# Attention scores turned onto pixels: fp32 products with a 0/1 matrix, or TensorE transposes with it

## The chip, the core and the metric

The kernel runs on one core of one Trainium2 chip, in one launch. The metric is the device time in microseconds (us) from the first to the last instruction. The engines are named as in the profile: PE is TensorE's matmul, PEld its weight load, DVE is VectorE, ACT is ScalarE, POOL is GpSimd, SP is the engine that issues most DMAs.

## The reference

The input is 16 images of 56 x 56 pixels with 384 channels, fp32. Two residual layers run over it:

```python
x = x + dilated_attention(_gn(x), w_qkv, w_proj, b_proj)
x = x + depthwise_conv(_gn(x), sign(w))      # 3 x 3, one filter per channel, signs of the weights
```

`_gn` is a group norm over 32 groups of 12 channels. The attention has 12 heads of 32 channels in three groups of four; group g looks at the 3 x 3 neighbours of each pixel at a distance of 1, 2 or 3. For each pixel and head that makes nine scores:

```python
attn = softmax(einsum('bgdn,bgdkn->bgnk', qg, ku) * scale)   # k: nine neighbours
out  = einsum('bgnk,bgdkn->bgnd', attn, vu)
```

## The kernel before

**Tiling.** Channels lie on partitions. An image is cut into 7 chunks of 8 rows, 448 pixels (`PX`), so there are 112 chunks. A chunk passes three stages: A (load, turn to channels-first, statistics), B (attention) and C (convolution, turn back, store). The three stages run at once on different chunks.

**Order.** Each piece of work is filed by `at(when, order, piece)` under a time slice and a rank in the slice; a chunk owns nine slices (`STEP`), and at the end (L856) all pieces are run in that order. The softmax ranks first in a slice, then scores, statistics, convolution, the weighing of values, queries, keys and values, the output product. This fixes the program's order. The queues in the trace depart from it in places: the compile-time scheduler places an instruction where it holds that its inputs are ready. On PE bursts are kept whole by `in_one_go`.

**Scores.** `query(g)` (L463) leaves 128 channels of queries in PSUM, `pq`. `score(i)` multiplies them on DVE by three shifted copies of the keys (L516, tile `t`). `score_rounds` (L501) sums the 32 channels of each head with a 0/1 matrix `sel`; its result `ps` has one partition per neighbour and head and 448 pixels along the row: neighbour p = 9 g + o lands on partitions 32 (p % 4) + 4 (p // 4) and the three after it.

**Softmax.** `softmax_1` copies `ps` to SBUF (`sT`, ACT, L533). Then PE brings 112 pixels at a time onto partitions (L536): four products, each with 112 columns of `sT` as the weights and the 0/1 matrix `permf` as the moving operand, all four into one PSUM bank, tile `pt_s`. `permf` also puts the 108 scores of a pixel into the order that the softmax wants (`place`). DVE takes the maximum (L541, `mx`), subtracts it (L542, into `ew`), ACT takes the exponential (L543). Later slices normalise (L547 to L549), split the weights into three bf16 terms and turn them back to rows by a transposing DMA (`aT`).

**Weighing.** `weigh(i)` spreads three weights over the 32 channels of their heads on PE (L582, `pb_a`, only one buffer), DVE multiplies by the values (L589, `w`), POOL adds up (L597, L600, L601). `out_project` (L615, `po`) is the output product; DVE adds bias and residual (L618).

**Buffers.** `pt_s`, `pkv`, `po`, `pc`, `pt_x`, `pt_o` and the small tiles of the norm share the three PSUM buffers of `ps_mt` under the tag `mt`; a new tile waits until the readers of the tile that had its buffer are done.

**Other transposes.** The kernel already has TensorE transposes: `pt_x` in stage A (L412) and `pt_o` in stage C (L799), both fp32 with the identity matrix as the moving operand. L799 has the same shapes as L536: weights of 128 x 112, moving operand of 128 x 128.

**The matrix.** `perm` is built once at the start by POOL (L104 to L110): 27 selects, one for each neighbour of each group, set four ones each. Five blocks of four columns stay zero.

Of the kernel before, what the change touches and what calls it, by code (L numbers as in the profile page):

```python
# [17 lines left out]
P = 128  # L18
HEADS = 4
HD = 32  # L20
NG = 3
NTAP = 9
NQ = 4
ROWS = 8
SUB = 112
# [3 lines left out]
NPAD = 32  # L29
# [6 lines left out]
def dilated_attention_then_binary_conv(  # L36
# [28 lines left out]
    nc = tc.nc  # L65
# [10 lines left out]
    def place(p):  # L76

        g, o = divmod(p, NTAP)
        return NG * o + g
# [22 lines left out]

    perm = const.tile([P, NPAD, HEADS], F32, name="perm")
    nc.gpsimd.memset(perm, 0.0)  # L104
    for p in range(NG * NTAP):
        v = place(p)
        nc.gpsimd.affine_select(
            out=perm[:, v, :], in_=perm[:, v, :], compare_op=ALU.not_equal, fill=1.0,
            base=-(32 * (p % 4) + 4 * (p // 4)), pattern=[[-1, HEADS]], channel_multiplier=1,
        )  # L110
    permf = perm.rearrange("p v h -> p (v h)")
# [333 lines left out]
    def plan_b(m, t0):  # L445
# [78 lines left out]
        def by_neighbour(ap):  # L524
            return ap.rearrange("p s (o k) -> p s o k", o=NTAP)

        def over_neighbours(ap):
            return ap.unsqueeze(2).to_broadcast([SUB, NSUB, NTAP, GH])

        def softmax_1():  # L530

            sT = s_p.tile([P, PX], F32, tag="sT", name="sT")
            nc.scalar.copy(sT, had.pop("ps")[:, :PX])  # L533
            pt = ps_mt.tile([P, 512], F32, tag="mt", name="pt_s")
            for s in range(NSUB):
                nc.tensor.matmul(  # L536
                    pt[:SUB, s * P : (s + 1) * P], sT[:, s * SUB : (s + 1) * SUB], permf, start=True, stop=True
                )
            pt4 = pt[:SUB].rearrange("p (s v) -> p s v", s=NSUB)[:, :, :NR]
            mx = s_p.tile([SUB, NSUB, GH], F32, tag="mx", name="mx")  # L540
            nc.vector.reduce_max(mx, by_neighbour(pt4).rearrange("p s o k -> p s k o"), axis=AX.X)  # L541
            nc.vector.tensor_tensor(by_neighbour(weights), by_neighbour(pt4), over_neighbours(mx), ALU.subtract)  # L542
            nc.scalar.activation(weights, weights, AF.Exp, scale=SCALE)  # L543
# [95 lines left out]
        for i in range(9):  # L639
            at(t0 + i, SCORE, lambda i=i: score(i))  # L640
        at(t0 + 9, SOFTMAX, softmax_1)
        at(t0 + 10, SOFTMAX, softmax_2)
        at(t0 + 11, SOFTMAX, softmax_3)
# [243 lines left out]
```

## Time and profile before

| | |
|---|---|
| median of 3 runs | 5411.35 us (5409.35 to 5414.15) |
| profiled execution | 5405.2 us, granted TensorE clock 0.98 |
| DVE busy | 4150.0 us (77%), 4209 instructions |
| ACT busy | 2397.8 us (44%) |
| POOL busy | 4215.2 us (78%) |
| DMA queues, share of 16 engines | 54.2% and under 1% each |
| L536, PE | 896 matmuls of 273 ns, first at 102.1 us, last at 5182.5 us |
| L536, weight loads | 896 of 177 ns |
| `pt_s` read by L541 and L542 on DVE | 112 each, 0.60 us and 0.59 us |
| from one chunk's L536 to the next | 44.88 us in the plainest chunks, up to 50.66 us |

A group's row in the profile names the line, the engine and the operation, then what it writes and reads with shapes, how often it ran, its busy time and the mean time of one. A time of one instruction is from its start to its modelled end; matmuls overlap, so how much of PE a burst takes is read from the starts: the start of the next burst less its own. PE shows twice as many matmuls on L536 (896) as the program has products (448): each fp32 product runs as two instructions. Each transpose of L799 and L412 runs as one (1344 in either line, which is what the program has).

The idle time before a group is given with what ended it. The engine and the semaphore of that releaser are in the trace; the instruction named is the last one of that engine before the wait ended, and is not always the one that was needed.

The page's chain of work that ended last explains only a few per cent of this span, so it carries little here.

### The profile page before, as it was taken

The page shows a single profiled execution, that of the slowest core. Times are in us where ns is not written, and L with a number is a line of the kernel's source. Part 1 is how long each engine was busy: PE and PEld are TensorE (multiplying, and loading weights), DVE is VectorE, ACT ScalarE, POOL GpSimd, SP SyncE. Part 2 cuts the span into 40 slices and gives each one's busy share as a digit, 9 for nine tenths or more (in the row PEclk, how much of TensorE's full clock was granted, in tenths as well). Part 3 has the DMA queues.
Part 4 walks back from the last instruction along what each step waited for, and adds up shares of the span by engine and source line. Part 5 has one row for each costly group of instructions (what it writes and reads, how often), then busy time and mean ns, then how long its engine had stood idle before and what let it go on. Part 6 is the DMA issues. An engine that isn't in the chain of part 4 may idle for free. (4 is left out here: it accounts for less than half of the span.)

```text
span 5405.2 us, 77297 instructions
## 1 busy us (share of the span) xinstructions
PE 5205.9 (96%) x27669; PEld 2414.4 (45%) x27669; DVE 4150.0 (77%) x4209; ACT 2397.8 (44%) x4189; POOL 4215.2 (78%) x3049
## 2 busy tenths in 40 slices
PE   8999999999999999999999999999999999999965
PEld 4444444444444444444444444444444444444422
DVE  4887777878777787777777777787777778777754
ACT  3224444444444444444444444444444444444433
POOL 2677888888888887888888788888888888888880
PEclk9999999999999999999999999999999999999976
DMA  5444555655555555555655655555555655544443
GB/s 168 127 120 124 159 157 158 163 154 161 158 158 160 164 159 159 157 157 158 163 154 161 164 152 160 164 157 163 159 157 154 164 154 161 161 130 134 122 130 126
DMA packets 810799, 825.73 MB, mean 153 GB/s; under 512 B 359467, under 2 KB 800174, under 8 KB 810414
## 3 DMA queue, kind: packets, MB, share of 16 engines
q1 hardware_dynamic: 802430, 808.79, 54.2%
q10 hardware_dynamic: 7984, 12.00, 0.7%
q8 instruction: 219, 3.59, 0.3%
q14 instruction: 166, 1.36, 0.1%
HBM read 466.41 MB, written 231.21 MB: 129 GB/s over the span
## 5 line engine op out<-in xcount | busy, mean ns | idle before, releaser
L597 POOL TENSOR_TENSOR w<-w 128x1344 f32<-128x1344 f32 x672 | 2049.9, 3050 | 456.2 <-DVE w L589 396.7
L589 DVE TENSOR_TENSOR w<-pb_a,v 128x1344 f32<-128x1344 f32 x1008 | 1559.1, 1547 | 267.0 <-PE pb_a L582 177.4
L516 DVE TENSOR_TENSOR t<-pq,k 128x1344 f32<-128x1344 f32 x1008 | 1535.8, 1549 | 237.0 <-PE pq L463 236.1
L463 PE MATMUL pkv<-xn,wqkvT 128*128 128x448 f32 x3924 | 1569.9, 549 | 9.0 <-ACT xa L424 4.7
L463 PEld LDWEIGHTS pkv<-xn,wqkvT 128*128 128x128 f32 x3924 | 718.4, 190 | 671.8 <-issue 629.4
L615 PE MATMUL po<-y,wprojT 128*128 128x448 f32 x2016 | 834.9, 550 | 27.4 <-POOL y L601 15.0
L784 POOL TENSOR_TENSOR m<-m 128x1344 f32<-128x1344 f32 x210 | 644.7, 3070 | 274.1 <-ACT m L778 274.0
L463 PE MATMUL pq<-xn,wqkvT 128*128 128x448 f32 x1962 | 830.7, 558 | 0.0
L713 ACT ACTIVATE z<-z,mrz 96x448 f32<-96x448 f32 x840 | 578.3, 751 | 350.9 <-DMA z<-x1d 330.3
L501 PE MATMUL ps<-t,sel 128*32 128x448 f32 x6048 | 666.0, 550 | 26.0 <-DVE t L516 25.3
L778 ACT ACTIVATE m<-zg,ktap 128x448 f32<-128x448 f32 x945 | 555.5, 658 | 274.0 <-POOL m L784 266.9
L615 PEld LDWEIGHTS po<-y,wprojT 128*128 128x128 f32 x2016 | 376.4, 191 | 382.9 <-issue 341.1
L727 PE MATMUL pc<-z,kdiag 96*32 96x440 f32 (+1 forms) x5040 | 516.7, 543 | 6.4 <-POOL z L715 4.6
L463 PEld LDWEIGHTS pq<-xn,wqkvT 128*128 128x128 f32 x1962 | 344.0, 189 | 316.9 <-issue 316.9
L734 DVE TENSOR_TENSOR x<-pc,x 128x448 f32<-128x448 f32 x224 | 139.3, 622 | 353.2 <-PE pc L727 342.1
L582 PE MATMUL pb_a<-aT,spread 24*128 24x448 bf16 x3024 | 369.1, 359 | 32.2 <-DVE w L589 25.9
L601 POOL TENSOR_TENSOR y<-y,w 128x448 f32<-128x448 f32 x336 | 381.5, 1135 | 22.6
L618 DVE SCALAR_TENSOR_TENSOR xr<-po,bias,xr 128x448 f32<-128x448 f32 x336 | 227.5, 677 | 220.9 <-PE po L615 217.2
L600 POOL TENSOR_TENSOR y<-w 128x448 f32<-128x448 f32 x336 | 382.2, 1138 | 14.7
L473 ACT COPY v<-pkv 128x448 f32<-128x448 f32 x336 | 178.3, 531 | 484.1 <-PE pkv L463 475.8
L473 ACT COPY k<-pkv 128x448 f32<-128x448 f32 x336 | 178.2, 530 | 376.5 <-PE pkv L463 376.5
L501 PEld LDWEIGHTS ps<-t,sel 128*32 128x32 f32 x6048 | 170.6, 110 | 364.9 <-issue 247.8
(131 smaller groups left out, 4394.7 us busy)
## 6 DMA issues: line engine op xcount, KB each, us to landing
z<-x1d SPq DMA_DIRECT2D x570, 224.0 KB
xr<-xd SPq DMA_DIRECT2D x112, 672.0 KB
x1d<-xr SPq DMA_DIRECT2D x112, 672.0 KB
xn<-xd SPq DMA_DIRECT2D x109, 672.0 KB
xin<-in_x_dram SPq DMA_DIRECT2D x108, 672.0 KB
xd<-xa SPq DMA_DIRECT2D x315, 224.0 KB
out_dram<-osb SPq DMA_DIRECT2D x420, 168.0 KB
x<-x1d SPq DMA_DIRECT2D x112, 448.0 KB
```

The source lines that it names most:

```text
L463: nc.tensor.matmul(dst[:, :PX], wqkvT[:, cc, o0 : o0 + P], had["xn"][:, cc, :], start=(cc == 0), stop=(cc == NG - 1))
L501: return nc.tensor.matmul(had["ps"][32 * j : 32 * j + 32, :PX], sel[:, s0 : s0 + 32], tk, start=(issued[j] == 1), stop=(issued[j] == len(r ...
L516: nc.vector.tensor_tensor(t.rearrange("p k (r w) -> p k r w", w=W), q3, k3, ALU.mult)
L589: nc.vector.tensor_tensor(w.rearrange("p k (r w) -> p k r w", w=W), pb[:, :, :PX].rearrange("p k (r w) -> p k r w", w=W), three(kv[1][g][m ...
L597: nc.gpsimd.tensor_tensor(w0, w0, w, ALU.add)
L600: nc.gpsimd.tensor_tensor(y, w0[:, 0], w0[:, 1], ALU.add)
L601: nc.gpsimd.tensor_tensor(y, y, w0[:, 2], ALU.add)
L615: nc.tensor.matmul(po[:, :PX], wprojT[:, g, j * P : (j + 1) * P], had[f"y{g}"], start=(g == 0), stop=(g == NG - 1))
L713: nc.scalar.activation(z, z, AF.Identity, bias=mrz[:, j, q, 0:1], scale=mrz[:, j, q, 1:2])
L727: return nc.tensor.matmul(pcr[q * HD : (q + 1) * HD, :, lo:hi], kdiag[:, kx, j * NQ + q, :], rows(set_of(j, q))[:, :, lo + kx - 1 : hi + k ...
L778: nc.scalar.activation(rows(t[:, kx]), zp[:, ky : ky + ROWS, kx : kx + W], AF.Copy, scale=ktap[:, o : o + 1])
L784: nc.gpsimd.tensor_tensor(had["m"], had["m"], t, ALU.add)
```

## The change

The four products per chunk become four TensorE transposes with the same two operands: `sT` as the data, `permf` in the place of an identity. A transpose passes values through,[...] the five blocks of columns that were zero get ones as well, on the 20 rows of `ps` that no neighbour uses. That is five selects more at the start. The aim is to spend fewer PE instructions on a step that only moves numbers.

```diff
-    for p in range(NG * NTAP):
-        v = place(p)
+    for p in range(NPAD):
+        v = place(p) if p < NG * NTAP else p
         nc.gpsimd.affine_select(
             out=perm[:, v, :], in_=perm[:, v, :], compare_op=ALU.not_equal, fill=1.0,
             base=-(32 * (p % 4) + 4 * (p // 4)), pattern=[[-1, HEADS]], channel_multiplier=1,
@@ softmax_1
             for s in range(NSUB):
-                nc.tensor.matmul(
-                    pt[:SUB, s * P : (s + 1) * P], sT[:, s * SUB : (s + 1) * SUB], permf, start=True, stop=True
-                )
+                nc.tensor.transpose(pt[:SUB, s * P : (s + 1) * P], sT[:, s * SUB : (s + 1) * SUB], permf)
```

## The prediction

> **What bounds the kernel now.** I first read the busy shares and the slices, then a table by stretches, to see where PE sets the pace.
>
> ```profile
> PE 5205.9 (96%) x27669; PEld 2414.4 (45%) x27669; DVE 4150.0 (77%) x4209; ACT 2397.8 (44%) x4189; POOL 4215.2 (78%) x3049
> PE   8999999999999999999999999999999999999965
> ...
> 214.00:4767.00 4553.00, 4494.65 (x24051) 2091.40 (x24050) 3612.33 (x3625) 2082.99 (x3641) 3711.38 (x2577) 1.00 0.57 156
> 5200.00:5405.00 205.00, 119.75 (x672) 46.73 (x672) 79.48 (x126) 70.73 (x118) 53.04 (x58) 0.64 0.41 127
> ```
>
> The columns of the last two rows are the stretch, its length, then PE, PEld, DVE, ACT, POOL, clock, DMA share and GB/s. From 214 to 4767 us PE is busy 98.7% (4494.65 of 4553) at full clock, DVE and POOL about 80%. PE is the bound there; only the last 205 us, where PE is busy 58%, belong to others. So PE time taken away counts, except where PE then waits.
>
> Next, the groups by shape, for the price of what goes and of what comes:
>
> ```profile
> L536 PE MATMUL pt_s<-perm,sT 128*112 128x128 f32 x896 | 116.4, 273 | 2.5 <-ACT sT L533 2.5
> L799 PE MATMUL pt_o<-ident,xg 128*112 128x128 f32 x420 | 115.3, 274 | 0.0
> L536 PEld LDWEIGHTS pt_s<-perm,sT 128*112 128x112 f32 x896 | 112.8, 177 | 46.2 <-issue 41.7 <-ACT sT L533 4.2 <-ACT z L713 0.2
> L799 PEld LDWEIGHTS pt_o<-ident,xg 128*112 128x112 f32 x420 | 56.2, 134 | 0.0
> ```
>
> A pass of a product and a transpose of the same shape both show 273 ns; only the weight loads differ, 177 against 134 ns. What differs is the count, 8 per chunk against 4. As matmuls overlap, what they take is read from the starts, in the timeline of a plain chunk:
>
> ```profile
> 2635.34 1.04 PE L536 MATMUL pt_s<-perm,sT 128*112 128x128 f32 x8
> 2636.30 0.36 PE L582 MATMUL pb_a<-aT,spread 24*128 24x448 bf16 x3
> ...
> 2641.60 0.39 PE L799 MATMUL pt_o<-ident,x 128*112 128x128 f32 x2
> 2641.82 0.27 PE L799 MATMUL pt_o<-ident,xg 128*112 128x128 f32 x1
> 2642.02 0.36 PE L582 MATMUL pb_a<-aT,spread 24*128 24x448 bf16 x3
> ...
> 2642.79 1.71 PE L501 MATMUL ps<-t,sel 128*32 128x448 f32 x16
> ```
>
> Columns: start, length, engine, group. In all 105 chunks between 200 and 5000 us whose start the timeline shows, the L536 burst takes 0.97 us to the next start.
>
> Last, what DVE does at the same time:
>
> ```profile
> 2633.28 3.02 DVE L516 TENSOR_TENSOR t<-pq,k 128x1344 f32<-128x1344 f32 x2 [0.82 <-PE pq L463]
> 2636.22 0.68 DVE L618 SCALAR_TENSOR_TENSOR xr<-po,bias,xr 128x448 f32<-128x448 f32 x1
> 2636.81 0.60 DVE L541 TENSOR_REDUCE mx<-pt_s 112x48 f32<-112x432 f32 x1
> ...
> 2640.64 1.55 DVE L516 TENSOR_TENSOR t<-pq,k 128x1344 f32<-128x1344 f32 x1
> ```
>
> DVE starts when `pq` is there, 2.06 us ahead of `pt_s`, and then works without a gap until about 2645. Its reader of `pt_s` starts 0.43 us after the burst's end (2635.34 + 1.04), behind other DVE work. DVE does not wait for `pt_s`.
>
> **What the Trainium skill says.** "TensorE: Matmul & The Clock Gate", Terms, says that transpose mode is 4x faster for FP32. The trace agrees only in part: the products are two passes, the transposes of the same shape one, at the same pace. I take 2x. Part 4 of the page, PE-mode transpose, gives about 275 ns for one in a kernel's context; L799 shows 274 ns. It also says that transposes don't count as busy for the clock gate; half a microsecond of them in 45 us should do nothing, and the clock is 1.00 in the stretch above with 24 other transposes in each chunk. Part 2, step 1, says weight loads run ahead under the matmuls; the trace agrees, since loads of 134 ns fit matmuls that start 110 ns apart.
>
> **The change part by part.**
> 1. Removed: eight passes. (1.04 - 0.273) / 7 = 0.110 us from start to start, plus 0.20 us from the last to `pb_a`: 0.97 us.
> 2. Added: four transposes. The starts of L799 lie 0.11 us apart (0.39 - 0.273 = 0.117 for a pair; 2641.60 to 2641.82 is two), and the last one leaves 0.20 us to `pb_a`: 3 x 0.11 + 0.20 = 0.53 us. Change of mode: `pkv` takes 4.61 us ahead of `pt_x` as elsewhere, so 0. PE saves **0.44 us** per chunk, 49 us in 112. The bounds are 0.40 and 0.50.
> 3. What follows on PE. The spread `pb_a` (L582) needs the last product `w`, done 3.84 us before; its next one at +6.69 us from `pt_s` has 2.1 us to spare. The first tile of `pkv` finds a free buffer. The trace puts the second `pkv` tile's weight load down to DVE's L542 in 91 chunks, but I take the name for chance: the load starts on its usual beat of 0.375 us, and in the first chunk the same load starts before L542 is done. By rotation of three buffers `pt_x` needs the one of `pt_s`, with 2 us to spare.
> 4. Where it can be lost. The burst of scores `ps` (L501) at 2642.79 needs the third product `t`, which DVE ends at 2642.19. Hand-over takes 0.05 us (seen wherever PE waits for it). Spare: 0.60 - 0.05 = 0.55 us, more than 0.44. As DVE is tied to `pq`, which comes ahead of the change, it ends `t` no sooner; after this burst it idles until PE's `pc` and moves with PE again. So I read this spare in each of the 112 chunks. **66 have 0.44 or more and keep all: 29 us. The others keep about 1 us together**: in the chunks without convolution (to about 500 us) and in one or two of seven chunks in each image `ps` already waits or has under 0.3 us, and in one of seven PE waits 0.46 to 0.88 us for the norm on POOL, 2.2 us after `pt_s`:
>
> ```profile
> PE ps L501 <- DVE t L516: 17.4, 25, 1.5
> PE pv L331 <- POOL dev L325: 9.9, 12, 0.9
> ```
>
> (us, times, longest, from 200 to 4700 us.) There the 0.44 us only lengthens the wait.
> 5. The five selects cost POOL 0.14 us each (27 took 3.84 us): 0.7 us at the start. PE begins at 7.15 us, when the input lands, so I take 0 and keep 0.7 as the other end. `perm` is first read at 101.7 us. Readers, copies and DMAs stay as they are.
>
> Sum: 29 + 1 = 30 us, 5411 - 30 = **5381 us**.
>
> **The rivals.**
> - B, nothing is lost: DVE's order moves so that `t` is ready in time, or waits on POOL shift along. Then 49 us: 5362. For it: DVE has 20% free. Against it: the waits on `pv` and `t` are there.
> - C, a wait takes its place: the second `pkv` tile does wait for L542. L542 ends 3.11 us after the old start of `pt_s`, the load starts at 3.25; with 0.05 us for the hand-over only 0.09 us is left of 0.44. 66 x 0.09 = 6 us: 5405. For it: the 91 entries. Against it: the first chunk.
> - D, slower: DVE's order is not the program's (two products `t` of later slices stand ahead of L618 and L541), so the compiler may regroup it when `pt_s` is ready sooner. If the reciprocal (0.36 us) and a statistic (0.48 us) come ahead of the third `t`, it ends 0.84 us later, `ps` starts at 6.91 + 0.84 = 7.75 us instead of 7.45, and 66 chunks lose 0.3 us: 20 us, 5431. For it: with 0.11 us of spare left nothing may move. Against it: the order repeats exactly from image to image.
>
> **How the numbers follow.** My forecast 0.52, B 0.15, C 0.18, D 0.15. A and B are faster by over 0.2% (10.8 us): 0.67. C is within it: 0.18. D: 0.15. The range reaches from B (with 0.7 us to it, and the pace's bounds) to just past C, 5359 to 5411, and leaves out D.
>
> **What would show it.** Right: L536 with 448 matmuls and loads of about 134 ns; the burst 0.53 us to `pb_a`; plain chunks 44.44 us apart instead of 44.88; `ps` at +7.01 us; the `pv` waits about 1.3 us; PE's waits for `t` longer by 0.44 us where they were. Wrong: transposes that start further apart than 0.12 us (step 2); a second `pkv` tile off its beat (step 3, C); `ps` waiting in plain chunks, or another order on DVE (step 4, D); a first transpose later than 7.2 us (step 5).

## The result, and the profile after

The changed kernel takes 5559.26 us (median of 4 runs, 5556.49 to 5564.79), against 5411.3 us for the kernel before on the same chip: a ratio of 1.0274, 95% interval 1.0256 to 1.0292. It is **148 us slower**, where 30 us less was forecast. The profiled execution spans 5557.5 us, the one before 5405.2 us. The three lines of the call in the softmax have become one, so from L537 on the line numbers of this profile are two below those of before; the kernels of the experiments have shifts of a few lines of their own.

From the page, the busy shares; then the row of the stretch from 214 to 4767 us, with the columns that the prediction explains:

```profile
PE 5227.1 (94%) x27221; PEld 2378.0 (43%) x27221; DVE 4154.6 (75%) x4209; ACT 2381.2 (43%) x4189; POOL 4224.4 (76%) x3054
```

```profile
214.00:4767.00 4553.00, 4382.79 (x22916) 1999.13 (x22914) 3510.85 (x3515) 2002.26 (x3527) 3607.00 (x2498) 0.98 0.56 152
```

PE has 448 instructions fewer, as it should, and yet 21.2 us more busy time (5227.1 against 5205.9). Its idle time over the whole span went from 199.3 to 330.4 us (span less busy time), 131 us more. The two make up the 152 us between the spans. In the stretch PE is busy 96.3% instead of 98.7%, and its granted clock is 0.98 instead of 1.00. So there are two questions: what PE waits for, and why fewer instructions take longer.

The edited operation itself did what was forecast. Its matmuls (count, least, median and longest in ns, first and last start), and a plain chunk in the timeline:

```profile
L536 PE MATMUL pt_s<-perm,sT x448: 272/273/323, 102.0 to 5324.5; 128*112 128x128 f32 x150
```

```profile
2633.28 0.60 PE L536 MATMUL pt_s<-perm,sT 128*112 128x128 f32 x4
2633.81 0.36 PE L580 MATMUL pb_a<-aT,spread 24*128 24x448 bf16 x3
...
2640.29 1.71 PE L501 MATMUL ps<-t,sel 128*32 128x448 f32 x16
```

The burst now takes 0.53 us to the next start (2633.81 - 2633.28, and the same in 99 of the 101 chunks between 200 and 5000 us; of the 105 bursts of before, 103 take 0.97 us and two 1.06), its weight loads 133 ns each, and `ps` starts at +7.01 us. The next chunk starts 44.44 us later. All four numbers stand in the prediction. But such a chunk comes about once in each group of seven; most others take 45 to 52 us. In the kernel before 38 of the 111 intervals are the plain 44.88 us; the longest is 53.15 us, not 50.66 as the table above has it.

What PE waited for between 200 and 5000 us (us in total, times, longest):

```profile
PE pkv L463 <- ACT xa L424: 59.6, 13, 4.6
PE pv L331 <- POOL dev L325: 49.6, 14, 3.9
PE ps L501 <- DVE t L516: 45.3, 50, 2.0
```

The same in the kernel before:

```profile
PE ps L501 <- DVE t L516: 19.8, 28, 1.5
PE pv L331 <- POOL dev L325: 10.8, 13, 0.9
PE pkv L463 <- ACT xa L424: 4.7, 1, 4.7
```

Two waits per group of seven chunks are new or long: one of 4.58 us of the keys and values (`pkv`) behind a copy, and one of 3.4 to 3.9 us of the norm (`pv`), which was at most 0.9 us. The waits of the scores for the product `t` grew too. Together the three wait 119 us more than before.

**How the long wait comes about.** Here is the chunk of the `pkv` wait in the timeline of the kernel before, cut to the path of the softmax weights:

```profile
1113.03 0.91 DVE L549 TENSOR_TENSOR ew<-ew,sm 112x432 f32<-112x432 f32 x1
...
1114.02 0.62 ACT L558 CAST e<-ew 112x512 bf16<-112x512 f32 x1 [0.79 <-ACT osb L801]
1114.40 1.54 DVE L589 TENSOR_TENSOR w<-pb_a,v 128x1344 f32<-128x1344 f32 x1
...
1119.24 1.16 POOL L559 TENSOR_TENSOR rest<-ew,e 112x512 f32<-112x512 f32 x1
...
1120.44 0.62 ACT L563 CAST e<-rest 112x512 bf16<-112x512 f32 x1 [5.42 <-POOL rest L559]
1120.96 0.52 ACT L424 COPY xa<-pt_x 128x448 f32<-128x448 f32 x1
...
1121.54 4.78 PE L463 MATMUL pkv<-xn,wqkvT 128*128 128x448 f32 x12
```

And the same place in the changed kernel:

```profile
1163.18 1.48 DVE L587 TENSOR_TENSOR w<-pb_a,v 128x1344 f32<-128x1344 f32 x1
...
1164.60 2.10 DVE L547 TENSOR_TENSOR ew<-ew,sm 112x432 f32<-112x432 f32 x1
...
1166.78 0.62 ACT L556 CAST e<-ew 112x512 bf16<-112x512 f32 x1 [3.35 <-issue]
1167.67 3.05 POOL L595 TENSOR_TENSOR w<-w 128x1344 f32<-128x1344 f32 x1
...
1172.86 1.14 POOL L557 TENSOR_TENSOR rest<-ew,e 112x512 f32<-112x512 f32 x1
...
1174.04 0.62 ACT L561 CAST e<-rest 112x512 bf16<-112x512 f32 x1 [6.64 <-POOL rest L557]
1174.56 0.53 ACT L424 COPY xa<-pt_x 128x448 f32<-128x448 f32 x1
...
1175.14 6.67 PE L463 MATMUL pkv<-xn,wqkvT 128*128 128x448 f32 x12 [4.59 <-ACT xa L424]
```

In the kernel before, DVE multiplies `ew` by the reciprocal and then takes the product `w` of the chunk before it. In the changed kernel `w` stands first. Measured from the chunk's `xr` (1106.65 and 1156.38 us), `ew` ends 3.0 us later (+10.3 instead of +7.3): 1.8 us because it starts later, and 1.2 us because it takes 2.10 us instead of 0.91, which the last section comes back to. ACT's cast is 3.0 us later, and on POOL a sum `w` of 3.05 us and a sum `y` now stand ahead of `rest`, so `rest` starts at +16.5 instead of +12.6. ACT waits 6.64 us for it with the copy `xa` queued behind; `xa` frees the PSUM buffer that `pkv` needs, and PE waits 4.59 us. ACT waited for `rest` before the change as well, 5.42 us, but then `xa` ended at 1121.48 us and `pkv` started at 1121.54 without a wait: there was nothing to spare. No instruction in this chain is one that the diff touches.

The swap is not a single case. The sixth product `w` of a chunk stands ahead of the next chunk's `ew` by `sm` in 97 of 111 places in the changed kernel and in 12 in the one before. As the long `pkv` wait comes only 13 times, the swap does not bring it everywhere.

The chunks without convolution at the start lose time through the same late `ew`: the weights' transposing DMA (`aT`) then lands later, and PE waits for it 16.1 us (6 times) between 100 and 480 us instead of 2.1 us (twice). The nine chunks up to there took 32 us more.

At the `pv` wait it is POOL's order that differs. In the chunk ahead of it, before and after:

```profile
1187.71 3.03 POOL L784 TENSOR_TENSOR m<-m 128x1344 f32<-128x1344 f32 x1 [3.51 <-ACT m L778]
1190.70 3.05 POOL L597 TENSOR_TENSOR w<-w 128x1344 f32<-128x1344 f32 x1
```

```profile
1237.30 3.05 POOL L595 TENSOR_TENSOR w<-w 128x1344 f32<-128x1344 f32 x1 [2.83 <-DVE pair L314]
1240.30 3.04 POOL L782 TENSOR_TENSOR m<-m 128x1344 f32<-128x1344 f32 x1
```

Before, the convolution's first sum `m` stood ahead of that sum `w`; now `w` stands first, and POOL waits 2.83 us for it. PE then waits 3.39 us for `dev` (L325), instead of 0.86 us.

**Why fewer instructions take longer.** In the last line of the fence above, 12 matmuls of `pkv` take 6.67 us. The same burst in the kernel before takes 4.78 us. By stretches around that wait (stretch, length, PE busy, granted clock, DMA share, GB/s):

```profile
1160.00:1170.00 10.00, 10.00 (x72) 1.00 0.47 146
1170.00:1175.10 5.10, 0.55 (x7) 0.71 0.01 1
1175.10:1177.00 1.90, 1.86 (x3) 0.50 0.00 0
1177.00:1179.00 2.00, 2.00 (x3) 0.51 0.21 42
1179.00:1181.80 2.80, 2.80 (x10) 1.00 1.10 256
```

After the idle 4.59 us PE runs at half its clock for some 4 us. In the changed kernel 27 full bursts of `pkv` between 500 and 5000 us are stretched in this way, by 1.4 to 3.0 us, 52.5 us together; each of them follows a wait of 3.39 us or more. The kernel before has two: one at 470 us around its wait of 4.73 us, and one at 5010 us around a wait of 2.84 us. Over all, PE is at half clock for 177.5 us between 200 and 5000 us, in 40 stretches; in the kernel before it is 23.9 us in 6. On average a `pkv` wait of 4.58 us costs 6.6 us, its burst's 2.0 us more counted in.

That closes the sum. The 448 instructions fewer are worth about 49 us of PE time, so with the 21 us more busy time some 70 us lie in slower matmuls: 56 in those of `pkv` and about 5 each in `ps`, `pq` and `po`. 131 us more idle time and 70 us in slower matmuls, less the 49 us, make the 152 us.

### The profile page after: what moved, and what is told of

Its sections match the earlier page's. It is cut to its first block, busy times and chain, and to the rows that moved or that the text cites. A ratio compares the mean times of both kernels' runs of the same rounds, so it can differ in the third digit from the quotient of the medians.

```text
span 5557.5 us, 76256 instructions
## 1 busy us (share of the span) xinstructions
PE 5227.1 (94%) x27221; PEld 2378.0 (43%) x27221; DVE 4154.6 (75%) x4209; ACT 2381.2 (43%) x4189; POOL 4224.4 (76%) x3054
## 4 chain that ended last, share of the span: by engine, by line
PE 52%; POOL 21%; DVE 8%; DMA 7%; ACT 6%; issue 4%; SPq 2%; POOLq 0%; ACTq 0%; DVEq 0%
PE pkv L463 18%; PE pq L463 9%; POOL m L782 7%; POOL w L595 7%; PE ps L501 7%; PE pc L725 6%; PE po L613 5%; POOL m L787 3%; ACT m L776 3%; DVE w L587 3%; DVE t L516 3%; PE pb_a L580 3%; PE pt_x L412 2%; PE pt_o L797 2%; ACT z L711 2%
## 5 line engine op out<-in xcount | busy, mean ns | idle before, releaser
L463 PE MATMUL pkv<-xn,wqkvT 128*128 128x448 f32 x3924 | 1627.9, 565 | 60.0 <-ACT xa L424 59.6
L463 PEld LDWEIGHTS pkv<-xn,wqkvT 128*128 128x128 f32 x3924 | 740.4, 196 | 752.5 <-issue 664.4
```

Source lines behind the costliest of these rows:

```text
L463: nc.tensor.matmul(dst[:, :PX], wqkvT[:, cc, o0 : o0 + P], had["xn"][:, cc, :], start=(cc == 0), stop=(cc == NG - 1))
```

## The experiments

The question was whether the loss lies in the transposes or in the order of everything else. The order on the queues is laid out when the program is compiled, and with transposes in place of products it comes out otherwise on every engine: taking each queue of the traces in order of start, by operation, tiles and shapes, and counting the lines of either kernel that have no match in the other, the two differ in 476 lines on DVE (of 4209 instructions in each), 286 on ACT, 495 on POOL (five of them the selects) and 446 of the DMAs that SP issues. On PE, taken by bursts, it is 90 (of some 4320). (The expectations quote counts from another listing, which differ a little.) Compiled with only the five selects more, nothing but the selects differs; with only the transposes, the order is that of the changed kernel. These two were compared as compiled and have no measured time.

**Transposes in the old order, and products in the new.** In `t_oldorder` the program is laid out with products, and the four instructions are turned into transposes once the order is fixed. `m_neworder` does the reverse. The selects are the 32 of the changed kernel in both. In the traces, `t_oldorder` has the order of the kernel before on DVE, ACT, POOL, SP and in PE's bursts, but for the five selects, and `m_neworder` has that of the changed kernel.

```diff
-                nc.tensor.transpose(pt[...], sT[...], permf)
+                turn = nc.tensor.matmul(pt[...], sT[...], permf, start=True, stop=True)
+                score_turns.add(turn.ins.name)
...
+    # after the order is fixed
+                if ins.name in score_turns:
+                    bb.instructions[k] = ins.__replace__(is_transpose=True)
```

> The transposes run in the order of the kernel before: the compiler fixes the order with products in place, and only then the four instructions of each chunk are turned into transposes. All engines' queues but for five selects at the start are those of before. Theory (the transposes are cheap, the new order of the other engines' queues costs the time): the prediction's sum holds, about 5381 us, plain chunks 44.44 us apart. Rival (the transposes themselves cost it, by a stall that single durations don't show): about 5559 us. A third possibility, a new wait in spite of the old order: about 5405 us.

Measured: 5385.47 us against 5410.39, ratio 0.9954 (0.9939 to 0.9968), faster than both kernels.

```profile
2625.28 0.60 PE L538 MATMUL pt_s<-perm,sT 128*112 128x128 f32 x4
...
2632.29 1.71 PE L503 MATMUL ps<-t,sel 128*32 128x448 f32 x16
```

That is a plain chunk of its timeline: `ps` at +7.01 us, without a wait, and the next chunk 44.44 us on, in nearly every plain chunk. Of 111 intervals between chunks 48 are shorter by 0.43 to 0.48 us. Two bursts of `pkv` are stretched, at the same places as in the kernel before.

> The reverse: the compiler fixes the order with transposes in place, then they are turned back into fp32 products. The queues are those of the changed kernel, the arithmetic that of before. Theory (the order costs the time): 5559 us or more, up to 5559 + 49 = 5608 us, as a chunk's burst takes 0.44 us more on PE where PE doesn't wait. Rival (the transposes cost it): back near 5411 us.

Measured: 5569.11 us, ratio 1.0294 (1.0278 to 1.0309). The two long waits of PE between 200 and 5000 us are there again, without a single transpose of scores:

```profile
PE pkv L465 <- ACT xa L426: 59.6, 13, 4.6
PE pv L333 <- POOL dev L327: 43.0, 14, 4.0
```

So **the order carries the whole loss**: 159 us with products (5569.11 - 5410.39), 174 us with transposes (5559.26 - 5385.47). The transposes save 25 us in the old order and about 10 us in the new one, where the two times were not taken together.

**Fewer transposes.** `t2of4` and `t1of4` keep two, and three, of the four products; the order is what the compiler lays out for each mix.

```diff
             for s in range(NSUB):
+                if s < 2:   # s < 1 in t1of4
+                    nc.tensor.transpose(pt[...], sT[...], permf)
+                    continue
+                nc.tensor.matmul(pt[...], sT[...], permf, start=True, stop=True)
-                nc.tensor.transpose(pt[...], sT[...], permf)
```

> Two of the four products of each chunk are transposes, two stay products; the compiler orders as it likes. It leaves DVE's queue nearly as before (36 of 3830 rows differ, against 499 with four transposes) and POOL's with 171 rows against 612. Theory (the order costs the time): PE saves 2 x 0.11 = 0.22 us in each chunk that keeps it, 66 x 0.22 = 15 us, so about 5396 us, give or take some 20 us for the rows that did move. Rival (the transposes cost it): half of the loss, about 5485 us.

Measured: 5468.26 us, ratio 1.0108 (1.0091 to 1.0125). This missed what I expected and lay nearer to the rival, a cost that grows with the number of transposes.

> One of the four products of a chunk is a transpose, three stay products, in the order the compiler lays out for that mix, in which two instructions on DVE stand elsewhere than in the kernel before. Main theory (the order sets the loss, the transposes themselves save a quarter of the 26 us that four save in the old order): 5404 us, give or take 6, a ratio of about 0.9988. Rival (a transpose costs something by itself that the old order hid, so that the loss grows with their number: a quarter of 148 us): 5448 us. With two transposes, in an order in which 36 instructions on DVE stand elsewhere, 5468 was measured.

Measured: 5453.10 us, ratio 1.0074 (1.0059 to 1.0089). Another miss, about 5 us from the rival's number. My expectation counted moved lines on DVE (2); but 26 on ACT, 78 on POOL and 108 of the DMA issues had moved too. Two runs in a row on the rival's side asked for a test with nothing else in it.

**One order, three mixes.** `m_1order` and `t_1order` have, on every queue, exactly the order of `t1of4`; the one holds four products, the other four transposes. The edit is that of `m_neworder` and `t_oldorder` over the loop of `t1of4`:

```diff
+                if s < 1:
+                    turn = nc.tensor.transpose(...)
+                else:
+                    turn = nc.tensor.matmul(...)
+                score_turns.add(turn.ins.name)
...
+                    bb.instructions[k] = ins.__replace__(is_transpose=None)   # True in t_1order
```

> All four stay products, on every queue in the order that the compiler laid out for one transpose and three products (5453.1 us with that mix). Main theory (the order carries the loss): 5453 plus the quarter of the 26 us that one transpose saved, so 5460 us, give or take 8. Rival (each transpose costs some 37 us by itself, a quarter of 148): without a transpose back to 5411 us.

> All four are transposes, on every queue in the order that the compiler laid out for one transpose and three products (5453.1 us with that mix). Main theory (the order carries the loss, transposes only shorten the burst): 5453 less three quarters of 26 us, so 5434 us, give or take 8. Rival (each transpose costs some 37 us by itself): 5559 us, as in the changed kernel.

Measured: 5455.73 us (ratio 1.0084, 1.0067 to 1.0101) with no transpose, 5438.60 us (1.0053, 1.0037 to 1.0068) with four, both within the 8 us allowed. The rival, at 5411 and 5559, falls: with more transposes the time goes down. That the three-product mix came near to a quarter of the loss was chance; its order loses 47 us by itself (5455.73 - 5408.35). For the mix with two transposes no such pair was run. `m_1order` shows where, between 200 and 5000 us:

```profile
PE po L621 <- ACT v L475: 31.9, 13, 3.8
PE pkv L465 <- ACT xa L426: 21.9, 14, 4.7
```

The kernel before waits 2.5 and 4.7 us for these. Both waits end with a copy on ACT, where only 26 lines moved; but POOL and the DMA queue moved as well, and no run parts them.

**Putting one instruction back.** `pin_dve` is the changed kernel with an order edge, no wait: DVE's sixth of the nine products of the weighing may not stand ahead of the next chunk's multiplication of `ew` by the reciprocal, which is the swap seen in the chain above.

```diff
+            scaled[m] = nc.vector.tensor_tensor(by_neighbour(weights), ..., over_neighbours(sm), ALU.mult)
...
+            if i == 5 and m + 1 in scaled:
+                behind(weighed, scaled[m + 1])   # order only
```

> The changed kernel with one order pinned per chunk: on DVE the sixth product of the weighing (L587, w) stays behind the softmax's last multiplication of the next chunk (ew by sm), as it stood before the change. An edge for the order alone, no wait. The other queues are ordered by the compiler anew. Theory A (this swap on DVE is the root: ew is late, so the bf16 terms on ACT, the remainder on POOL and the copies behind them on ACT are late): most of the 148 us comes back, 5380 to 5430 us. Theory B (POOL's order around the batch's norm and the convolution's sums is what costs): little comes back, 5500 us or more.

Measured: 5460.15 us, ratio 1.0093 (1.0077 to 1.0108): 99 of the 148 us come back, which lies between the two theories. Its longest sums of waits on PE:

```profile
PE pv L339 <- POOL dev L333: 48.0, 14, 3.6
PE pb_a L590 <- DVE w L597: 40.7, 27, 3.7
```

In its trace the sixth product never stands ahead (0 of 111). The `pkv` wait is gone and the chunks at the start take 40.37 us instead of 42.5 to 44.2 (before: 39.46). The `pv` wait is still there, and with it 14 stretched bursts of `pkv`, nearly one for each group, 32.7 us together. The edge moved more than the swap: against the changed kernel 298 lines on DVE and 518 on POOL stand elsewhere. So it is shown that the `pkv` wait goes with this edge, but not that the swap alone is worth the 99 us.

`pin_pool` sets an edge on POOL instead: the first sum `w` of the weighing (`i == 1`) behind the convolution's sum `m` of the middle row of taps. In the traces the sum `w` stands ahead of that `m` in 33 of 105 places before the change, in 60 in the changed kernel and in none with this edge, so the edge goes further than the old order; so does that of `pin_dve`, with 0 instead of 12. `pin_both` has both edges.

```diff
+            added = nc.gpsimd.tensor_tensor(w0, w0, w, ALU.add)
+            if i == 1:
+                tapped[m] = added
...
+                tap = nc.gpsimd.tensor_tensor(had["m"], had["m"], t, ALU.add)
+                if ky == 1 and m + 8 in tapped:
+                    behind(tapped[m + 8], tap)
```

> The changed kernel with one more order edge and no new wait: on GpSimd the sum of the weighing's second pair (the `w` of `weigh`, i = 1) may not be put ahead of the convolution's addition `m` of the middle row of taps in the chunk of the same time; the edge moves other instructions of the compile-time order too. Main theory (the time lost lies in places where one queue's new order makes a queue behind it wait, and each place can be named): the 14 waits of PE's `pv` for GpSimd's `dev`, 49.6 us in 200 to 5000 us, fall to about 10 to 15 us as in the kernel before, the 59.6 us of `pkv` behind the copies `xa` stay, and the time is 5525 us, give or take 15. Rival (GpSimd's order is a symptom, `dev` is late because DVE hands over later): the `pv` waits stay above 35 us and the time is within 10 us of 5559.

> The changed kernel with both order edges: DVE's last weighing product behind the next chunk's multiplication of `ew` by `sm`, and GpSimd's sum of the weighing's second pair behind the convolution's `m`. Main theory: with the `pkv` waits gone as with the first edge alone (5460.15 us) and the `pv` waits down by some 35 us, 5425 us, give or take 20; 5386, the time of the four transposes in the old order, is the floor. Rival (each edge only moves the loss to another queue, since the orders were laid out together): within 15 us of 5460 or above it, with a new wait of over 20 us on PE in place of the `pv` one.

Measured: `pin_pool` 5646.59 us, ratio 1.0429 (1.0414 to 1.0445), the slowest of all; `pin_both` 5519.32 us, 1.0196 (1.0179 to 1.0213). The first is outside both of its forecasts, and the second missed my 5425. In `pin_pool` the waits on `dev` did fall, to 7.9 us, but these stand in their place:

```profile
PE pb_a L588 <- DVE w L595: 69.1, 43, 4.6
...
PE pb_a L588 <- DMA aT<-e: 55.3, 19, 4.0
```

In `pin_both` the `pb_a` wait for `w` grew to 76.4 us, from 40.7 in `pin_dve`, while the one on `dev` fell to 22.5. So my theory held in that the named wait shrinks, and failed in that the time does not follow: the rival of `pin_both`, that each edge moves the loss to another queue, is what happened. The edge also moved other instructions (334 lines on POOL and 214 on ACT against the changed kernel), so it is no clean measure of the `pv` wait. What that wait is worth alone stays open; that it makes up the 49 us left in `pin_dve` is only argued.

## Why the prediction was wrong, step by step

- **Steps 1 and 2 held.** 448 matmuls of 273 ns, 0.11 us apart, 0.53 us to `pb_a`, loads of 133 ns. "TensorE: Matmul & The Clock Gate", Terms, has transposes 4x faster for FP32; the trace shows half the passes at the same pace, so 2x was the right reading.
- **Step 3 held.** In the old order the plain chunk takes 44.44 us, so the full 0.44 us arrives: the second `pkv` tile does not wait for L542, and rival C is out.
- **Step 4 held in the old order, with its term too large.** 48 chunks kept the 0.44 us, not 66: 21 us instead of 29. The other intervals gain up to 3.4 us or lose up to 2.6, 4 us net, so the chunks sum to 24.5 us and the run to 25 us, where the step gave 30. As forecast, the longest `pv` wait grew to 1.3 us.
- **Step 5 has two parts.** The last select starts 0.70 us later (6.41 instead of 5.71 us), as forecast. The first weight load starts at 7.62 instead of 7.15 us; but with the same 32 selects it starts at 6.84 us in `m_neworder` and at 7.89 us in `pin_both`, so no cost of the selects can be read from it. The selects make `permf` a full permutation; no run leaves them out under transposes. The sentence after it, "Readers, copies and DMAs stay as they are", **is the step that failed**. They stayed in the program, but not in the queues: the step put the new order at nothing, and it costs 174 us with transposes and 159 with products.
- **Rival D had the right kind of cause and the wrong size.** It let the compiler regroup DVE near the third `t`, by 0.84 us, and counted 0.3 us in 66 chunks: 20 us, with a chance of 0.15. What moved was the order on DVE, ACT, POOL and the DMA queue, and what was lost was only in part on `t` (25.5 us more waiting); the most went to two waits of 3.4 to 4.6 us in each group of seven chunks, and to the clock after them. Its argument against, "the order repeats exactly from image to image", shows a fixed order for one program and says nothing on the next program's. Its argument for, that DVE's order is not the program's, was the one to follow to the end: if the compiler chose this order, it may choose another for any edit that changes an instruction of the loop. With one possible order out of many in hand, the range should have reached far above D.
- **The term that no step had** is the clock. I used the page's clock gate only to say that transposes would not lower it. Its Part 1 also says that an idle stretch of about 3.4 us brings the half clock. The traces agree only in part. In the eleven profiles together, between 200 and 5000 us, all 94 waits of PE of 3 us or more were followed by it (a mean granted clock under 0.9 over the next 4 us), but so were 90 of the 120 between 2 and 3 us and 69 of the 330 between 1 and 2 us. What sets the shorter ones apart is open. The forecast brought no new wait of 3 us, so the price was never needed; a rival with such waits would have needed it.

## What to carry to other kernels

When a compile-time scheduler lays out the queues, the swap of one instruction for a cheaper one is two changes: the instruction, and a new order for all engines. Price them apart: fix the old order and put the new instruction in. Here that gave -25 us, while the new order cost +174 us. In a loop where PE is busy 98.7%, look first for instructions that stand in another order, then for what is queued behind them; and price a PE wait of over 3 us at more than its length, since in these traces the clock fell after each of them. An edge that puts one instruction back may win or lose, as the other queues are laid out anew with it: one brought 99 us back here, another cost 87 us more.

## What I had not expected of the hardware

- The half clock after a wait: 12 matmuls of `pkv` in 6.2 to 7.8 us instead of 4.78 us. It is not a sharp bound on the last wait alone: in `m_neworder` bursts are stretched after waits of 2.96 us, in `pin_pool` eight after waits of 1.58 to 2.67 us, in `m_1order` one after 1.31 us.
- `ew` by the reciprocal took 2.10 us in the fence above and 0.60 us in the median; its longest was 3.22 us. Here it ran beside a POOL sum of 3.04 us that started at 1163.19 us, and ended 0.47 us after it. The two traces tell when it is long. In the changed kernel 83 of these multiplications start while POOL runs nothing; they take 0.58 to 0.61 us. 27 start while a POOL instruction has more than 0.13 us still to run, up to 2.75 us: every one of them ends 0.46 to 0.48 us after that instruction's end. In the kernel before the same holds for 10 and for 59. "SBUF — State Buffer", in the section on its two separate sides, says that DVE with two SBUF inputs and GpSimd lock each other out of a shared port for a whole instruction. The times of both traces agree; the port itself they don't show. So a moved instruction can also grow by what it now stands beside: this one by 1.2 of the 3.0 us that it came late.
